# A graph layer with a mixture of experts on one core: a chunk of four windows moved from the end of the chunk list to its front, a short chain for every chunk of four, weights loaded in order of use, slot work per edge tile capped

## Chip, cores and metric

One NeuronCore of a Trainium2 chip runs the whole program in one launch. The metric is the device time of one execution in microseconds (us), median of the timed runs. Beside the timed runs one further execution was recorded by the hardware profiler; all durations of single instructions come from it.

## What is computed

6250 nodes with 256 features each, 100,000 edges sorted by destination, 8 experts of which each node uses 2. Cut to what matters:

```python
h = layernorm(x)
agg = segment_sum(h[src], dst) / max(deg, 1)            # mean over incoming edges
x = x + concat([h, agg], axis=1) @ gnn_W.T + gnn_b
xn = layernorm(layernorm(x)) * gamma + beta
logits = xn @ Wr + br
w = softmax(top_k(logits, 2))                           # two experts for each node
for e in range(8):
    y += (gelu(xn @ W1[e] + b1[e]) @ W2[e] + b2[e]) * w_full[..., e]
x = x + y
```

All data and all matmuls are fp32. The expert matrices are 256 x 512 and 512 x 256.

## The kernel before, in words

**Early stage.** The kernel first computes, for all nodes, a matrix `z_d` (normalised features times the neighbour half of the graph weights, with 8 router columns) and then, in steps spread over the first edge tiles (`u_stages`), `u_d` (the own half, with the residual). Both are kept in DRAM.

**Edge phase.** The sorted edges are cut into W = 56 windows of C = 14 edge tiles of P = 128 edges, 784 tiles in all. For an edge tile, POOL gathers the 128 source rows of `z_d` into one of XG = 16 `xg` tiles (`gather`, L594); DVE makes a one-hot matrix of the destinations for seven tiles at a time (`hot_tiles`, L605); PE adds the tile into the window's sums with one fp32 matmul, which the records show as two (`add_edges`, L611). Gathers are written 16 tiles ahead, so a gather waits only until the matmul 16 tiles before it has released its `xg` tile. A window's first row may be shared with the window before it: the sums go to DRAM and one row comes back (`put_sums`, `share_row`), and DVE adds it (`shared_row`, L617).

**From sums to expert slots.** Four windows make a group. When a group's sums are there, a fixed chain of steps runs on DVE, ACT and PE: normalisation, router logits, rank of the experts, one-hot slots (`one_hot_slots`, L686/L687), a matmul that sorts the tokens (`sort_tokens`, L694), and for the chunk the positions of each window's run of tokens of each expert (`share_runs`, `place_runs`, `tile_experts`). ACT then copies the runs into a slot buffer `xe` (`copy_runs`, L809); there are two of them, taken in turn, and each is cleared once by DVE when it is first used (L797). At which edge tile after the group's end each step is written is set by the class `Steps`: there is a long form and a short form. In the long form the copies begin 37 tiles after the last window and the experts (`placed`) 50 tiles after it for a chunk of four windows, 62 for a chunk of eight; in the short form they begin 23 and 32 tiles after it for a chunk of four. Only the last two chunks use the short form.

**Chunks and experts.** The windows are grouped into chunks of TG = 4 or CW = 8 windows. A chunk is what the experts work on at a time. With eight windows each expert has 256 slots, with four 128, and one slot task then takes two experts; three extra tiles of 128 slots (XT) take what doesn't fit. `expert_stages` returns a chunk's slot tasks as a list of (planned us, function): `hidden` (L825, 1.8 or 2.0 us), `result` (L840, 1.75 us), and `one`, `two`, `three` (L857, L866, L875; 1.7, 0.5 and 1.75 us) for the extra tiles. Results go to `y_d` in DRAM.

**The order of the work** on all engines is that of the program, written by hand[...]. `after(t)` is called behind each edge tile t. It writes the steps that fall due at t, then takes slot tasks from the list `tasks` until the budget `rate` (planned us per edge tile) is used up, then lets `sum_rows` write row sums. `start_experts` sets `rate` when a chunk's experts become ready: the planned us in the list divided by the tiles left until the chunk's `deadline`. When the last chunk becomes ready, the rate is 2.0. After the last edge tile the same function is called with t = 784, 785 and so on until nothing is left.

**Row sums.** `sum_rows` gathers, for one window, each token's two expert results from `y_d` with two POOL gathers (`gather_rows`, L923), and later (6 planned us later, or when more than four wait) adds them on DVE (`add_rows`, L930) and stores the rows. It begins in the last 100 edge tiles, one window for every 12 planned us, faster in the last 16 tiles; after the last edge tile it is one window for every 2.4 planned us, but a window only once its chunk's slot tasks have all been written. From the last 16 tiles on, the row sums use the `xg` tiles as buffers.

**Weights.** When the last step of `u_stages` has been written (edge tile 38), its memory is given to the pool `slots`, and the 16 weight loads of 512 KB (eight of `w1`, then eight of `w2`) are issued on ACT's queue, one for every two tiles from tile 40.

The chunk list is one line (L77), the planner's parameters one line each:

```python
sizes = [TG] + [CW] * ((W - 4 * TG) // CW) + [TG] * 3
...
nw, short = chunks[index][1], index >= len(chunks) - 2
...
rate = max(rate, 1.01 * total / (deadline(L.index) - now))
...
spent = min(spent + rate, rate) if tasks else 0.0
```

Of the kernel before, what the change touches and what calls it, by code (L numbers as in the profile page):

```python
# [8 lines left out]
F32 = mybir.dt.float32  # L9
# [8 lines left out]
P = 128  # L18
EPS = 1e-5
C = 14  # L20
TB = 4
UB = 2
TG = 4
CW = 8
# [7 lines left out]
def gnn_ffn_kernel(ctx: ExitStack, tc: tile.TileContext, x, x_cols, src, dst, gw, gw_t, gb, gb_cols, gamma, beta,  # L32
# [30 lines left out]
    nc = tc.nc  # L63
    N, D = x.shape
    E = src.shape[0]
    NX, H = w1.shape[0], w1.shape[2]
    KD, KH = D // P, H // P
# [3 lines left out]
    W = -(-E // EW)  # L71
# [2 lines left out]
    DZ = D + NX  # L74
    DA = DZ + 1
    HR = NT * P
    sizes = [TG] + [CW] * ((W - 4 * TG) // CW) + [TG] * 3  # L77
    assert sum(sizes) == W
    chunks = [(sum(sizes[:i]), n) for i, n in enumerate(sizes)]

# [8 lines left out]
    def slot_number(nw):  # L89
        return more_at(nw) + XT * P  # L90

    SC = slot_number(CW) + CAP
# [410 lines left out]
    def weights(pool):  # L503
        w1_sb = pool.tile([P, NX, KD, H], F32, name="w1_sb", bufs=1)
        w2_sb = pool.tile([P, NX, KH, D], F32, name="w2_sb", bufs=1)
        parts = [(w1_sb[:, e], w1[e].rearrange("(k p) h -> p k h", p=P)) for e in range(NX)]
        parts += [(w2_sb[:, e], w2[e].rearrange("(k p) d -> p k d", p=P)) for e in range(NX)]
        return w1_sb, w2_sb, parts

    xg = [edges.tile([P, DA], F32, name=f"xg{i}") for i in range(XG)]  # L510
# [97 lines left out]
    def add_edges(V, c):  # L608
        if c == 0:
            V.pS = ps.tile([P, DA], F32, name="pS")  # L610
        nc.tensor.matmul(V.pS, V.hot[c // HC][:, c % HC, :], xg[(V.g * C + c) % XG],  # L611
                         start=(c == 0), stop=(c == C - 1))
# [179 lines left out]
    def copy_runs(K, e, j0, nw):  # L792
        if e == 0 and j0 == 0:
            assert K.index < 2 or Ks[K.index - 2].left == 0
            if K.index < 2:
                xe.append(slots.tile([P, KD, SC], F32, name=f"xe{K.index}", bufs=1))
                nc.vector.memset(xe[-1], 0.0)  # L797
            K.xe = xe[K.index % 2]
        _, v = nc.values_load_multi_w_load_instructions(
            K.runs[0:1, e, j0:j0 + nw, :].rearrange("o j t -> o (j t)"), engines=(ET.Activation,),  # L800
            min_val=0, max_val=slot_number(K.nw), skip_runtime_bounds_check_because="clamped to it")
        for i in range(nw):
            j = j0 + i
            src_at = nc.s_assert_within(v[2 * i + 1], 0, 2 * P,
                                        skip_runtime_bounds_check_because="a window has so many at most")
            whole = xs[:, j * KD * 2 * P:(j + 1) * KD * 2 * P + CAP]
            src = bass.AP(tensor=whole.tensor, offset=whole.offset,
                          ap=[whole.ap[0], [2 * P, KD], [1, 2 * P + CAP]])
            nc.scalar.activation(K.xe[:, :, bass.ds(v[2 * i], CAP)], src[:, :, bass.ds(src_at, CAP)], AF.Copy)  # L809

    def expert_stages(K):

# [126 lines left out]
    tasks, later, xe, Ks, sums, adds = [], {}, [], [], [], []  # L939
    slots, w1_sb, w2_sb = None, None, None  # L940
    now, spent, rate, clock, due, spares = None, 0.0, 0.0, 0.0, 0.0, 0
    ends = [(first + n) * C - 1 for first, n in chunks]

    class Steps:
# [1 line left out]


        def __init__(self, index):
            nw, short = chunks[index][1], index >= len(chunks) - 2
            if short:  # L950
                self.x1, self.var, self.roots, self.norms = 2, 4, 5, 7
                self.route, self.exps, self.weigh, self.choices, self.count = 8, 10, 11, 12, 14
                self.hot, self.sort, self.each, self.tiles, self.copied, self.pace = 17, 20, 1, 17, 23, 1
            else:
                self.x1, self.var, self.roots, self.norms = 3, 6, 8, 11
                self.route, self.exps, self.weigh, self.choices, self.count = 12, 15, 17, 18, 22
                self.hot, self.sort, self.each, self.tiles, self.copied, self.pace = 25, 29, 2, 27, 37, 1.5
            self.placed = self.copied + int(NX * nw // TG * self.pace) + 1
# [3 lines left out]
    def deadline(index):  # L962

        if index + 1 == len(chunks):
            return None
        t = ends[index + 1] + steps_of[index + 1].placed
        if chunks[index][1] > chunks[index + 1][1] or index == len(chunks) - 3:
            t = ends[index + 2] + steps_of[index + 2].copied - 4
        return t

    def at(t, f, *args):
        later.setdefault(max(t, now), []).append(lambda: f(*args))
# [36 lines left out]
    def start_experts(K):  # L1009
        nonlocal rate  # L1010
        tasks.extend(expert_stages(K))
        Ks.append(K)
        rate, total = 0.0, 0.0
        for L in Ks:
            total += sum(us for us, _, of in tasks if of is L)
            if L.left and deadline(L.index):
                rate = max(rate, 1.01 * total / (deadline(L.index) - now))
        if K.index == len(chunks) - 1:
            rate = 2.0
        sums.extend((K, j) for j in range(K.nw))  # L1020

    def sum_rows():

        nonlocal due
        while adds and (adds[0][0] <= clock or not (sums or tasks)):
            adds.pop(0)[1]()
        left = W * C - 1 - now
        while sums and not sums[0][0].left and clock >= due and left < 100:
            if 0 < left < XG and spares + 3 > XG - left:
                return  # L1030
            K, j = sums.pop(0)
            V = Group()
            gather_rows(K, j, V)
            adds.append((clock + 6.0, lambda K=K, j=j, V=V: add_rows(K, j, V)))
            while len(adds) > 4:
                adds.pop(0)[1]()
            due = clock + 12.0 if left >= XG else max(due, clock - 6.0) + (4.0 if left > 0 else 2.4)

    def after(t):
        nonlocal now, spent, clock  # L1040
        now = t
        while later.get(t):
            later[t].pop(0)()
        later.pop(t, None)
        clock += 0.6 if t < W * C else 0.3
        spent = min(spent + rate, rate) if tasks else 0.0
        while tasks and spent > 0:
            us, f, _ = tasks.pop(0)
            spent -= us
            clock += us  # L1050
            f()
        sum_rows()

    def new_window(g, V_before):
        V = Group()
        V.g, V.before, V.hot = g, V_before, []
        hot_tiles(V, 0)
        return V
# [7 lines left out]
    for index, (first, nw) in enumerate(chunks):  # L1066
        K = Group()
        K.index, K.first, K.nw, K.groups = index, first, nw, []
        K.count = work.tile([1, 2, CW, NX], F32, name="count")
        for g in range(first, first + nw):  # L1070
            if g % TG == 0:
                G = Group()
                G.n, G.first, G.x1 = TG, g, []
                G.mv = small.tile([P, TG, 2], F32, name="mv4", bufs=2)
                K.groups.append(G)
            if g > 0:
                V = V_next
            for c in range(C):
                t = g * C + c
                add_edges(V, c)  # L1080
                if c == 0:
                    hot_tiles(V, HC)
                if c == HC and g + 1 < W:
                    V_next = new_window(g + 1, V)
                if t + XG < len(edge_tiles):
                    gather(*edge_tiles[t + XG])
                for to, what in loads[:1]:
                    loads.pop(0)
                    nc.sync.dma_start(to, what)
                if u_tasks and t % 2 == 0:  # L1090
                    u_tasks.pop(0)()
                    if not u_tasks:
                        u_pools.close()
                        slots = fast_pools.enter_context(tc.tile_pool(name="slots", bufs=2))
                        w1_sb, w2_sb, parts = weights(slots)
                        for n, (to, what) in enumerate(parts):
                            at(t + 2 + 2 * n, nc.scalar.dma_start, to, what)
                if c == HC + 5:
                    load_u(V)
                if c == C - 1:  # L1100
                    window_done(V, G, K, t)
                after(t)
    t = W * C
    while later or tasks or sums or adds:
        after(t)
        t += 1
# [8 lines left out]
    with tc.If(wrong_r > 0), tc.tile_pool(name="gp", bufs=1) as gp:  # L1115
        w1_sb, w2_sb, parts = weights(gp)
# [130 lines left out]
```

## Time and profile before

| What | us |
|---|---|
| timed runs, median of 3 (lowest, highest) | 1456.79 (1456.22, 1457.76) |
| the profiled execution's own time | 1251.55 |
| its span, first to last instruction | 1249.6 |
| PE busy with matmuls | 1081.8 (87%) |
| POOL busy | 866.3 (69%) |
| first and last edge gather (L594) | 72.4 and 1087.5 |
| first and last edge matmul (L611) | 83.6 and 1112.5 |
| last slot matmul begins (L875) | 1222.9 |

The profiled execution is 205 us shorter than the median of the timed runs. A time inside the program can only be read from the profiled one. A line of a group of instructions gives the source line, engine, operation, output and input by their names, the count, the busy time and the mean duration of one in ns, then the idle time of the engine just before these instructions and what ended most of it. "issue" means that the profile shows nothing that was waited for. A line of a timeline gives start, duration and instruction, and in brackets the idle time before it and what ended it. The granted clock is that of PE, 1.00 being full speed; its mean in this execution was 0.95.

### The profile page before, as it was taken

What the parts mean: (1) busy time and instruction counts of PE and PEld (TensorE: products, weight loads), DVE (VectorE), ACT (ScalarE), POOL (GpSimd) and SP (SyncE); (2) the same over time, 40 slices, a digit from 0 to 9 for tenths busy, and PEclk for the clock granted to TensorE, in tenths of its full rate; (3) what the DMA queues carried; (4) which work ended last, traced back from release to release, by engine and by line L of the source; (5) the groups of instructions that cost most, each with busy time, mean ns of one, the idle gap of its engine ahead of it and who ended that gap; (6) DMA issues with size and microseconds to landing.
All of it is one profiled execution on the core that took longest, in us unless ns stands there. A gap on an engine that the chain in (4) does not pass through costs nothing. (4 is left out here: it accounts for less than half of the span.)

```text
span 1249.6 us, 17771 instructions
## 1 busy us (share of the span) xinstructions
PE 1081.8 (87%) x4806; PEld 869.3 (70%) x4806; DVE 684.6 (55%) x2137; ACT 446.0 (36%) x1155; POOL 866.3 (69%) x915
## 2 busy tenths in 40 slices
PE   6998746787869999999999999899999898997881
PEld 5877535665648887677768777787768776885670
DVE  6766647543746276634746275534734647348452
ACT  2510003521273236433373236433363424433520
POOL 3057777777777777777777777777777776656672
PEclk9999978898999999999999999999999998998896
DMA  9989895455554555555555555555555665656673
GB/s 287 350 293 310 268 363 135 129 155 137 142 144 135 155 157 156 150 148 144 151 152 150 151 145 156 146 152 143 150 152 151 165 179 138 159 174 198 199 222 108
DMA packets 140272, 221.74 MB, mean 177 GB/s; under 512 B 23316, under 2 KB 107615, under 8 KB 140038
## 3 DMA queue, kind: packets, MB, share of 16 engines
q0 software_dynamic: 43104, 120.94, 37.3%
q1 hardware_dynamic: 88726, 90.15, 22.2%
q10 hardware_dynamic: 8336, 9.45, 2.2%
q8 instruction: 41, 0.67, 0.2%
q14 instruction: 65, 0.53, 0.1%
HBM read 166.29 MB, written 54.20 MB: 176 GB/s over the span
## 5 line engine op out<-in xcount | busy, mean ns | idle before, releaser
L594 POOL DMA_INDIRECT xg<-z_d,src_i x784 | 745.0, 950 | 287.5 <-issue 115.7
L611 PE MATMUL pS<-xg,hot 128*128 128x265 f32 x1568 | 441.9, 404 | 63.1 <-DMA xg<-z_d,src_i 35.7
L611 PEld LDWEIGHTS pS<-xg,hot 128*128 128x128 f32 x1568 | 294.3, 196 | 156.7 <-DMA xg<-z_d,src_i 69.7
L825 PE MATMUL ph<-xe,w_sb 128*128 128x256 f32 (+1 forms) x1152 | 226.9, 349 | 23.9 <-ACT xe L809 23.9
L825 PEld LDWEIGHTS ph<-xe,w_sb 128*128 128x128 f32 x1152 | 193.3, 203 | 47.7 <-ACT xe L809 26.8
L840 PE MATMUL py<-w_sb,hid 128*128 128x256 f32 x896 | 213.0, 382 | 4.4 <-DVE rows L844 4.3
L840 PEld LDWEIGHTS py<-w_sb,hid 128*128 128x128 f32 x896 | 170.2, 191 | 30.7 <-DVE rows L844 6.4
L832 ACT ACTIVATE hid<-ph,b_sb 128x256 f32<-128x256 f32 (+1 forms) x288 | 103.4, 426 | 234.3 <-PE ph L825 234.1
L605 DVE TENSOR_TENSOR hot<-cols,rel 128x896 f32<-128x896 f32 x112 | 121.0, 1081 | 86.8 <-PE pS L611 84.1
L809 ACT ACTIVATE xe<-xs x448 | 139.4, 311 | 62.8 <-ACT xe L809 31.0
L923 POOL DMA_INDIRECT xg<-y_d,rows_i x92 | 89.1, 969 | 60.2 <-issue 20.9
L697 ACT ACTIVATE xs<-pm,beta_sb,gamma_sb 128x256 f32<-128x256 f32 x112 | 57.1, 561 | 112.0 <-PE pm L694 112.0
L844 DVE TENSOR_TENSOR rows<-py,b_sb 128x512 f32<-128x512 f32 x56 | 38.5, 688 | 97.6 <-PE py L840 97.6
L621 ACT ACTIVATE sums<-pS 128x265 f32<-128x265 f32 x56 | 21.7, 388 | 167.8 <-issue 56.4
L617 DVE TENSOR_TENSOR pS<-pS,row 1x265 f32<-1x265 f32 x55 | 23.4, 426 | 92.4 <-PE pS L611 76.7
L694 PE MATMUL pm<-to,xn 128*128 128x256 f32 x224 | 59.0, 387 | 10.5 <-DVE end L757 4.9
L256 PE MATMUL ph<-gc,x_t 128*128 128x264 f32 (+1 forms) x200 | 57.5, 413 | 10.5 <-DVE u_t L415 6.3
L930 DVE SCALAR_TENSOR_TENSOR xg<-xg,w,xg 128x256 f32<-128x256 f32 x92 | 44.0, 483 | 38.6 <-DMA xg<-y_d,rows_i 22.2
L857 PE MATMUL ph<-w_sb,xe 128*128 x108 | 56.5, 649 | 7.2 <-DVE rows L861 6.7
L832 ACT ACT_TABLE_LOAD x23 | 29.5, 1283 | 79.8 <-PE ph L825 79.5
L875 PE MATMUL py<-w_sb,hid 128*128 x216 | 52.2, 385 | 6.1 <-ACT hid L869 3.3
L694 PEld LDWEIGHTS pm<-to,xn 128*128 128x128 f32 x224 | 42.1, 192 | 20.6 <-issue 12.8
(190 smaller groups left out, 919.5 us busy)
## 6 DMA issues: line engine op xcount, KB each, us to landing
y_d<-rows SPq DMA_DIRECT2D x56, 256.0 KB
xg<-z_d,src_i POOLq DMA_INDIRECT x784, 2.9
w_sb<-w_dram ACTq DMA_DIRECT2D x16, 512.0 KB
sums_d<-sums SPq DMA_DIRECT2D x55, 132.5 KB
x<-u_d SPq DMA_DIRECT2D x55, 132.0 KB
x_d<-x SPq DMA_DIRECT2D x56, 128.0 KB
u_d<-u_t SPq DMA_DIRECT2D x24, 264.0 KB
x_t<-x_cols_dram SPq DMA_DIRECT2D x12, 512.0 KB
```

What stands on the lines that cost most here:

```text
L256: nc.tensor.matmul(pz, x_t[:, t, k, :], gc[:, h * KD + k, :n], start=(k == 0), stop=(k == KD - 1))
L594: nc.gpsimd.indirect_dma_start(out=xg[(g * C + c) % XG][:, :DZ], out_offset=None, in_=z_d[:, :], in_offset=bass.IndirectOffsetOnAxis(ap=sr ...
L605: nc.vector.tensor_tensor(hot, col[:, None, :].to_broadcast([P, HC, P]), V.rel[:, c:c + HC, None].to_broadcast([P, HC, P]), op=ALU.is_equal)
L611: nc.tensor.matmul(V.pS, V.hot[c // HC][:, c % HC, :], xg[(V.g * C + c) % XG], start=(c == 0), stop=(c == C - 1))
L694: nc.tensor.matmul(px[:, k, :], G.xn[i][:, k * P:(k + 1) * P], G.one_hot[i], start=True, stop=True)
L697: nc.scalar.activation(xs[:, at:at + 2 * P], px[:, k, :], AF.Identity, bias=beta_sb[:, k:k + 1], scale=gamma_sb[:, k:k + 1])
L809: nc.scalar.activation(K.xe[:, :, bass.ds(v[2 * i], CAP)], src[:, :, bass.ds(src_at, CAP)], AF.Copy)
L825: nc.tensor.matmul(ph[:, i, a * S:(a + 1) * S], w1_sb[:, U.e + a, k, c * P:(c + 1) * P], K.xe[:, k, (U.e + a) * S:(U.e + a + 1) * S], star ...
L832: nc.scalar.activation(U.hid[:, c, a * S:(a + 1) * S], ph[:, i, a * S:(a + 1) * S], AF.Gelu, bias=b1_sb[:, U.e + a, c:c + 1])
L840: nc.tensor.matmul(U.py[:, h, :], U.hid[:, c, h * P:(h + 1) * P], w2_sb[:, U.e + h * UE // 2, c, :], start=(c == 0), stop=(c == KH - 1))
L857: nc.tensor.matmul(ph, K.xe[:, k, at:at + P], w1_sb[:, bass.ds(T.e, 1), k, :].rearrange("p a h -> p (a h)"), start=(k == 0), stop=(k == KD ...
L923: nc.gpsimd.indirect_dma_start(out=V.y2[r], out_offset=None, in_=y_d[K.index][:, :], in_offset=bass.IndirectOffsetOnAxis(ap=G.rows[:, r, i ...
```

## The change

The chunk list becomes two chunks of four, five of eight, two of four; before it was one of four, five of eight, three of four. Every chunk of four uses the short form of `Steps`. The weight loads are issued in the order w1[0], w1[1], w2[0], w1[2], w2[1] and so on, on the same queue behind the same tiles. The two clears of the slot buffers leave `copy_runs` and are written 4 and 12 tiles behind the end of `u_stages`. The rate is limited to 0.72 planned us per edge tile, and behind the last edge tile the budget is 2.0 per step from the start.

```diff
-    sizes = [TG] + [CW] * ((W - 4 * TG) // CW) + [TG] * 3
+    sizes = [TG] * 2 + [CW] * ((W - 4 * TG) // CW) + [TG] * 2
...
-        parts = [(w1_sb[:, e], w1[e].rearrange("(k p) h -> p k h", p=P)) for e in range(NX)]
-        parts += [(w2_sb[:, e], w2[e].rearrange("(k p) d -> p k d", p=P)) for e in range(NX)]
+        first = [(w1_sb[:, e], w1[e].rearrange("(k p) h -> p k h", p=P)) for e in range(NX)]
+        second = [(w2_sb[:, e], w2[e].rearrange("(k p) d -> p k d", p=P)) for e in range(NX)]
+        parts = first[:1]
+        for e in range(NX):
+            parts += first[e + 1:e + 2] + second[e:e + 1]
...
     def copy_runs(K, e, j0, nw):
         if e == 0 and j0 == 0:
             assert K.index < 2 or Ks[K.index - 2].left == 0
-            if K.index < 2:
-                xe.append(slots.tile([P, KD, SC], F32, name=f"xe{K.index}", bufs=1))
-                nc.vector.memset(xe[-1], 0.0)
             K.xe = xe[K.index % 2]
...
+    def clear_slots():
+        xe.append(slots.tile([P, KD, SC], F32, name=f"xe{len(xe)}", bufs=1))
+        nc.vector.memset(xe[-1], 0.0)
...
-            nw, short = chunks[index][1], index >= len(chunks) - 2
+            nw, short = chunks[index][1], chunks[index][1] < CW
...
-                rate = max(rate, 1.01 * total / (deadline(L.index) - now))
-        if K.index == len(chunks) - 1:
-            rate = 2.0
+                rate = max(rate, 1.01 * total / max(1, deadline(L.index) - now))
+        rate = min(rate, 0.72)
...
-        spent = min(spent + rate, rate) if tasks else 0.0
+        pace = rate if t < W * C else 2.0
+        spent = min(spent + pace, pace) if tasks else 0.0
...
                         for n, (to, what) in enumerate(parts):
                             at(t + 2 + 2 * n, nc.scalar.dma_start, to, what)
+                        for n in range(2):
+                            at(t + 4 + 8 * n, clear_slots)
```

## The prediction

> **Words used.** An edge tile is one of the 784 groups of 128 edges; the kernel is written tile by tile, and behind each tile go some "slot tasks" (the expert matmuls of an earlier chunk). Windows are the 56 groups of 14 tiles. "Units" are the planner's own microseconds for slot tasks (`expert_stages`), 510.7 in all: 41.85 for a chunk of 4 windows, 68.65 for one of 8. The tail is what is written behind the last edge tile, in steps numbered on from 784.
>
> **What bounds the kernel now.** I read the page's engine line and groups first, then the busy time by stretches, then POOL's timeline near the end, then the waits after the last edge tile.
>
> ```profile
> PE 1081.8 (87%) x4806; PEld 869.3 (70%) x4806; DVE 684.6 (55%) x2137; ACT 446.0 (36%) x1155; POOL 866.3 (69%) x915
> ...
> L594 POOL DMA_INDIRECT xg<-z_d,src_i x784 | 745.0, 950 | 287.5 <-issue 115.7
> L611 PE MATMUL pS<-xg,hot 128*128 128x265 f32 x1568 | 441.9, 404 | 63.1 <-DMA xg<-z_d,src_i 35.7
> ...
> L923 POOL DMA_INDIRECT xg<-y_d,rows_i x92 | 89.1, 969 | 60.2 <-issue 20.9
> ```
>
> PE looks like the bound, but POOL's 69% leaves out the 0.30 us ahead of each gather. The stretches show it (columns: us, then busy time and instructions of PE, PEld, DVE, ACT, POOL, then clock, DMA share, GB/s).
>
> ```profile
> 150.00:200.00 50.00, 28.49 (x96) 21.34 (x95) 27.15 (x94) 6.24 (x13) 37.85 (x40) 0.76 0.91 303
> ...
> 800.00:850.00 50.00, 48.71 (x224) 41.70 (x223) 22.02 (x58) 13.71 (x28) 37.81 (x40) 1.00 0.55 150
> ...
> 1050.00:1100.00 50.00, 48.74 (x268) 41.15 (x267) 24.85 (x77) 23.57 (x76) 30.71 (x33) 1.00 0.56 150
> ...
> 1200.00:1250.00 50.00, 19.22 (x72) 13.12 (x70) 16.94 (x35) 3.43 (x12) 21.29 (x23) 0.76 0.51 151
> ```
>
> POOL makes 40 gathers per 50 us, one per 1.25 us, from 100 us to 1000 us without a break, whether PE is busy (800) or not (150). So POOL paces the edge phase, and PE work can be moved about in it for nothing. At 1050 POOL is down to 33: there PE holds it. POOL's timeline says where:
>
> ```profile
> 1087.52 0.95 POOL L594 DMA_INDIRECT xg<-z_d,src_i  x1 [0.30 <-PE pS L611]
> 1089.65 0.95 POOL L923 DMA_INDIRECT xg<-y_d,rows_i  x1 [1.19 <-PE pS L611]
> ...
> 1104.88 0.96 POOL L923 DMA_INDIRECT xg<-y_d,rows_i  x1 [2.11 <-PE pS L611]
> ...
> 1110.52 0.94 POOL L923 DMA_INDIRECT xg<-y_d,rows_i  x1 [2.17 <-PE pS L611]
> ...
> 1229.23 0.94 POOL L923 DMA_INDIRECT xg<-y_d,rows_i  x1 [11.55 <-DMA y_d<-rows]
> ```
>
> The last edge gather is at 1087.5, the last edge matmul at 1112.5 (its line's last start): PE is 25 us behind, and the row-sum gathers into the same `xg` tiles wait for it. Then the tail, POOL at one gather per 1.25 us again up to 1217, and the last chunk: its experts start at 1174.7, PE ends at 1224.9, the last four windows' gathers go at 1229 to 1239.
>
> [...] the next gather follows by 0.30 us, while the y gathers land 3.6 us (median) after issue. So 1.25 us is POOL's own time. [...] the tail shows "DVE xg <- DMA xg<-y_d" for 22.2 us. [...]
>
> **The change part by part.** The total is unchanged: four chunks of 4 and five of 8 either way, so no matmul, gather or copy is added. Units are honest: a `result` of 1.75 units shows 8 matmul records in 1.73 us, a two-expert `hidden` of 2.0 shows 1.78; a chunk of 4 is about 39.7 us of PE, one of 8 about 67.4, so 0.95 to 0.98 of the units.
>
> *Where slot work goes.* I worked the rates through by the code's own formulas. Before: experts start at tile 105 at 0.34 units a tile; from 229 0.62; from 677 1.0; from 759 1.27. By the last edge tile 431.0 units are done, 37.9 are queued and 41.9 come with the last chunk. After: start at 87 with the cap 0.72, from 143 0.30, from 285 0.62, from 733 0.72. Done by tile 676: 325.3 against 316.5; by the last edge tile 395.7, so 73.2 queued plus 41.9. The head start is 8.8 units; beyond that, 35.3 units move from the last 100 edge tiles into the tail.
>
> *Start.* An earlier start at 87 to 143 costs PE 0.445 (edge tile) + 0.70 + 0.085 (sort) = 1.23 us a tile, under POOL's 1.25: nothing, hidden by POOL. The 16 weight loads keep ACT's queue and tiles 40 to 70, only their order changes; the first need (about 195 us) comes after their issue (149 to 179 us): nothing. The two clears (L797, 4.3 us each) move from tiles 92 and 204 to 42 and 50 on DVE, ahead of the one-hot tiles, where DVE already waits 11.1 us for a row. Behind them queue L617 and L605, and PE behind these. Cover is the 16 gathered tiles, 20 us: I take 0, the other end +9. The short chain puts chunk 0's and 1's DVE and ACT steps into 32 steps in place of 50; PE and DVE have room (28 and 27 of 50 us), 0.
>
> *Edge phase end.* POOL unhindered, with 20 row-sum gathers among the edges (10 windows): 72.4 + 783 x 1.25 + 20 x 1.25 = 1076; measured 1087.5, so 11 us were PE's doing. After: 9 windows by the same arithmetic, PE at 1.23 never behind: 1074 for the last gather, 1078 for the last edge matmul. That is 35 us early.
>
> *Tail.* PE has 35.3 units x 0.97 = 34 us more in it. Taken by PE alone: 1078 + 62.9 units until step 815 (61) + sort and counts (5) = 1144 for the last chunk's start, + 52 units (50) + some 5 idle = 1199. But POOL: 94 row-sum gathers are left, in place of 92, and 34 windows are written between tile 777 and step 815. The add follows about three windows later: 31 x 2.5 + 1.25, plus stalls like the 12 us of before (76 gathers from 1110.5 to 1217.7 took 107 in place of 95) in proportion, 9, plus landing 3.6: 1075 + 91 = 1166 before DVE is through to the copies. (The same sum for before: 1110.5 + 50 + 6 + 3.6 = 1170; measured 1174.7.) Windows go on to step 825: DVE there at about 1075 + 106 + 12 + 4 = 1197, PE one item (about 5 us) ahead, then 32 units (31 us) without row sums. PE ends between 1192 + 31 = 1223 and, if adds hold it less, 1213; I take 1219 for 1224.9. The drain after it (24.7 us: last writes, eight gathers, store) stays.
>
> **Sum.** -6 us: 1251.6 to about 1245.6 in the profiled execution. The median of the timed runs is 1456.8, 205 us above the profiled one, and no view shows why. I carry the difference over in us, since both explanations I can price keep it near: if the 205 us lie outside the loop, -6 stays. If PE ran at some 0.75 of its clock, PE would bound tiles 285 to 784: the edge phase saves 44.1 units (those done from 677 on) x 0.97 / 0.75 = 57, the early stretch costs 7 (56 tiles at 1.64 in place of 1.25, minus what 229 to 285 gets back), the tail grows by 45: -5. So **1451**.
>
> **Rivals.** (a) *PE free of POOL in the tail*: adds don't hold PE; end at 1199 in place of 1224.9, -26, **1431**. For it: py and rows buffers let PE lead a little; against: before's start at 1174.7 fits POOL's sum. (b) *Slower: POOL is the timed runs' bound.* If the 205 us lie in the 896 gathers (0.23 us each, 1.48 in all), POOL's pace with row sums is 1.8 us a tile, above even before's 1.5 to 1.76 of PE: there is no 25 us backlog to remove, the last edge comes 3 us earlier only, and 34 us of PE work plus three windows stand behind the row sums: after 31 units at the end in place of 12, and three windows x 3.0: +28, **1485**. It decides once the backlog that the cap removes is under about 28 us; the profile has 36 (25 + 11). (c) *Same*: DVE is at 1197 as worked out and PE finishes at 1223 to 1226: **1456**, within 0.2%. (d) *Early stall*: the clears delay the one-hot tiles until POOL's 16 tiles run out, +9 less the gain: **1460**.
>
> **Chances.** Forecast, 1440 to 1453.8: 0.47; (a) 0.12; (c) 0.17; (d) and like small losses 0.12; (b) 0.12. A difference of 0.2% (2.9 us) is about what this measurement can tell from none. Faster 0.59, same 0.17, slower 0.24. The forecast's own range is 1440 to 1453.8; the range that leaves out (b) and the far end of (a) is 1437 to 1470.
>
> **What would show it.** Right: last L594 near 1074 and last L611 within 5 us of it; POOL 40 per 50 us up to there; no "<-PE pS L611" ahead of the first L923; experts of the last chunk from about 1165; PE busy nearly without a gap after 1197; drain as before. Wrong: POOL under 40 per 50 us around 150 to 200 (clears); the last edge matmul well after 1080 (PE behind at 0.72); last chunk's start near 1175 or later.

## The result, and the profile after

| | before | after |
|---|---|---|
| timed runs, median of 4 each | 1456.51 us (1442.55 to 1457.76) | 1476.55 us (1465.74 to 1482.05) |

The ratio is 1.0144, with a 95% interval of 1.0095 to 1.0192: 20 us slower, where 6 us faster was forecast.

The 205 us between the profiled execution of before and its timed runs belong to the chip on which a kernel runs: the unchanged kernel takes 1457 us on one chip (A below; by their times, the timed runs above and the profile named "after" come from it) and 1251 us on another (B). On B the changed kernel takes 1279.72 us against 1251.80, ratio 1.0219 (1.0189 to 1.0248), which is +28 us. So profiles are compared here only between chips of the same pace. The profile shown of before stands for B; on which chip it was made isn't known, but the profile of `loads_clears` below, made on B and as fast as before, has the same four stages to about 1 us. The page of after on A:

```profile
PE 1156.3 (78%) x4806; PEld 916.2 (62%) x4806; DVE 683.7 (46%) x2137; ACT 444.4 (30%) x1155; POOL 865.8 (59%) x915
...
L597 POOL DMA_INDIRECT xg<-z_d,src_i x784 | 745.6, 951 | 472.5 <-issue 173.8
L614 PE MATMUL pS<-xg,hot 128*128 128x265 f32 x1568 | 447.9, 417 | 47.2 <-issue 39.0
```

and of the same kernel on B (line numbers are those of the changed kernel, 3 or 4 higher than before's):

```profile
PE 1088.4 (85%) x4806; PEld 866.8 (68%) x4806; DVE 684.2 (54%) x2137; ACT 446.0 (35%) x1155; POOL 867.3 (68%) x915
...
L597 POOL DMA_INDIRECT xg<-z_d,src_i x784 | 746.0, 952 | 303.2 <-issue 115.2
L614 PE MATMUL pS<-xg,hot 128*128 128x265 f32 x1568 | 446.9, 407 | 76.3 <-DMA xg<-z_d,src_i 53.5
...
L927 POOL DMA_INDIRECT xg<-y_d,rows_i x94 | 91.0, 969 | 72.9 <-DMA y_d<-rows 30.3
```

The counts are those of before but for two row-sum gathers (94 for 92, and two fewer into `y`), and the busy times too: no work was added. On B the idle time before the edge gathers grew from 287.5 to 303.2 us. The busy time by stretches says where (B, the windows shown of before and the one ahead of them):

```profile
100.00:150.00 50.00, 42.19 (x172) 33.54 (x171) 35.12 (x94) 0.79 (x2) 34.75 (x37) 0.95 0.85 264
150.00:200.00 50.00, 27.91 (x89) 20.77 (x87) 35.86 (x104) 5.96 (x12) 35.24 (x38) 0.78 0.91 301
...
1050.00:1100.00 50.00, 44.91 (x191) 37.96 (x192) 30.77 (x105) 22.29 (x60) 37.81 (x41) 0.90 0.58 158
...
1200.00:1250.00 50.00, 44.16 (x249) 36.86 (x249) 18.50 (x37) 13.12 (x47) 19.34 (x21) 0.97 0.50 156
```

POOL makes 37 and 38 gathers in the first two, where before it made 40; at 1050 it makes 41, where before it was held down to 33; at 1200 PE is still at work, where before it was nearly done. POOL's timeline at the two joints of the tail:

```profile
1098.37 0.95 POOL L597 DMA_INDIRECT xg<-z_d,src_i  x1 [0.31 <-issue]
1099.62 0.95 POOL L927 DMA_INDIRECT y<-y_d,rows_i  x1 [0.30 <-DMA xg<-z_d,src_i]
...
1257.30 0.94 POOL L927 DMA_INDIRECT xg<-y_d,rows_i  x1 [29.00 <-DMA y_d<-rows]
```

The wait for PE ahead of the first row-sum gather is gone, as forecast, but the last edge gather comes at 1098, not at 1074. Cut at edge gathers 285 and 677 (counted from 0), the last edge matmul and the last slot matmul, the time goes as follows (us in each stage, the first of them from the first edge gather on, read off POOL's and PE's timelines; the last two cuts are the starts of the last group of each):

| stage | before, B | after, B | difference | before (`b0`), A | after, A | difference |
|---|---|---|---|---|---|---|
| gathers 0 to 285 | 361.0 | 381.3 | +20.3 | 414.8 | 434.8 | +20.0 |
| gathers 285 to 677 | 491.0 | 491.5 | +0.5 | 577.4 | 576.5 | -0.9 |
| gather 677 to last edge matmul | 188.1 | 166.0 | -22.1 | 219.5 | 201.4 | -18.1 |
| to last slot matmul | 110.4 | 141.3 | +30.9 | 138.2 | 167.1 | +28.9 |

Both chips say the same: 20 us are lost at the start, and the end loses 9 to 11 where it should have won 6. (On A a single execution scatters: the profiled one of `b0`, the kernel before run once more, took 1451.7 us, its median is 1459.5.)

### The profile page after: what moved, and what is told of

Read it like the earlier page. It is cut to its first block, busy times and chain, and to the rows that moved or that the text cites. A ratio compares the mean times of both kernels' runs of the same rounds, so it can differ in the third digit from the quotient of the medians.

```text
span 1479.5 us, 17770 instructions
## 1 busy us (share of the span) xinstructions
PE 1156.3 (78%) x4806; PEld 916.2 (62%) x4806; DVE 683.7 (46%) x2137; ACT 444.4 (30%) x1155; POOL 865.8 (59%) x915
## 5 line engine op out<-in xcount | busy, mean ns | idle before, releaser
L597 POOL DMA_INDIRECT xg<-z_d,src_i x784 | 745.6, 951 | 472.5 <-issue 173.8
L614 PE MATMUL pS<-xg,hot 128*128 128x265 f32 x1568 | 447.9, 417 | 47.2 <-issue 39.0
L614 PEld LDWEIGHTS pS<-xg,hot 128*128 128x128 f32 x1568 | 317.2, 206 | 131.2 <-issue 69.2
L829 PE MATMUL ph<-xe,w_sb 128*128 128x256 f32 (+1 forms) x1152 | 232.8, 351 | 48.5 <-ACT xe L809 19.6
L844 PE MATMUL py<-w_sb,hid 128*128 128x256 f32 x896 | 237.2, 407 | 34.3 <-issue 30.7
L844 PEld LDWEIGHTS py<-w_sb,hid 128*128 128x128 f32 x896 | 182.8, 206 | 69.3 <-issue 34.5
L809 ACT ACTIVATE xe<-xs x448 | 139.3, 311 | 60.2 <-issue 29.5
L697 PE MATMUL pm<-to,xn 128*128 128x256 f32 x224 | 66.4, 420 | 49.9 <-DVE to L690 16.4
L879 PE MATMUL py<-w_sb,hid 128*128 x216 | 60.5, 430 | 30.8 <-DVE rows L883 20.6
L861 PE MATMUL ph<-w_sb,xe 128*128 x108 | 61.7, 701 | 28.5 <-DVE rows L865 19.5
L879 PEld LDWEIGHTS py<-w_sb,hid 128*128 128x128 f32 x216 | 44.8, 215 | 43.5 <-ACT xe L809 17.8
```

The lines of the kernel that those rows point to most:

```text
L597: nc.gpsimd.indirect_dma_start(out=xg[(g * C + c) % XG][:, :DZ], out_offset=None, in_=z_d[:, :], in_offset=bass.IndirectOffsetOnAxis(ap=sr ...
L697: nc.tensor.matmul(px[:, k, :], G.xn[i][:, k * P:(k + 1) * P], G.one_hot[i], start=True, stop=True)
L829: nc.tensor.matmul(ph[:, i, a * S:(a + 1) * S], w1_sb[:, U.e + a, k, c * P:(c + 1) * P], K.xe[:, k, (U.e + a) * S:(U.e + a + 1) * S], star ...
L844: nc.tensor.matmul(U.py[:, h, :], U.hid[:, c, h * P:(h + 1) * P], w2_sb[:, U.e + h * UE // 2, c, :], start=(c == 0), stop=(c == KH - 1))
L861: nc.tensor.matmul(ph, K.xe[:, k, at:at + P], w1_sb[:, bass.ds(T.e, 1), k, :].rearrange("p a h -> p (a h)"), start=(k == 0), stop=(k == KD ...
L879: nc.tensor.matmul(py[:, 0, :], T.hid[:, c, :P], w2_sb[:, bass.ds(T.e, 1), c, :].rearrange("p a d -> p (a d)"), start=(c == 0), stop=(c == ...
```

## The experiments

Two theories of the loss stood at first. *Start*: the early slot work of the first chunk makes PE wait in front of the edge matmuls, POOL's 16 tiles run out, and every later gather shifts. *Tail*: what the cap pushes behind the last edge tile costs more than it saves. A third, that the loss belongs to the chip, had to go first. `rate`, `placed`, `short` and `sizes` are those of the diff. Each run is compared with the kernel before on its own chip.

### On chip A: is it the chip, and is it the cap?

`b0` is the kernel before, unchanged.

> The kernel before, unchanged, to have its profile in the condition of its timed runs (about 1456 us) and not only the 1251 us one. Ratio to itself 1.00. If PE's waits of the kind 'issue' come with that condition and not with the change, they are some 300 to 400 us here too (74 us in the 1251 us profile, 360 us in the changed kernel's). If the change brings them, they stay under 100 us and the time under 1300.

Measured: 1459.51 us, ratio 1.0008 (0.9982 to 1.0034). `chunks_only` is before with the new list and the short chain:

```diff
-    sizes = [TG] + [CW] * ((W - 4 * TG) // CW) + [TG] * 3
+    sizes = [TG] * 2 + [CW] * ((W - 4 * TG) // CW) + [TG] * 2
...
-            nw, short = chunks[index][1], index >= len(chunks) - 2
+            nw, short = chunks[index][1], chunks[index][1] < CW
```

> Only the chunk list and the short chain of the kernel after; weights, clears and budget as before. Theory START (the early, short chain of the first chunk stalls the edge tiles): slower than before by 10 to 25 us. Theory TAIL (the cap moves 34 us of PE work behind the last edge tile, where it isn't hidden): within 0.4% of before.

Measured: 1480.55 us, 1.0156 (1.0108 to 1.0203). `after_nocap` is after with before's budget:

```diff
-        rate = min(rate, 0.72)
+        if K.index == len(chunks) - 1:
+            rate = 2.0
...
-        pace = rate if t < W * C else 2.0
-        spent = min(spent + pace, pace) if tasks else 0.0
+        spent = min(spent + rate, rate) if tasks else 0.0
```

> The kernel after with the budget rule of before (no cap at 0.72, 2.0 only once the last chunk is ready). START: as slow as the kernel after, +15 to +25 us on before, the clears adding up to 9 of them. TAIL: within 0.4% of before, since the last edge tiles again take the slot work.

Measured: 1472.51 us, 1.0105 (1.0066 to 1.0144). `after_again` is the changed kernel.

> The kernel after, on the same chip as the three others: +1.0% to +1.9% on before, as in the first measurement.

Measured: 1478.80 us, 1.0154 (1.0103 to 1.0204). So the loss is there without cap, clears and weight order (`chunks_only`), and stays without the cap (`after_nocap`). What the cap is worth on A can't be told: the intervals of 1.0105 and 1.0154 overlap.

What chip A's profiles have more of is waits. PE's waits of before on B, then of after on A (us in all, times, longest):

```profile
PE pS L611 <- issue: 7.2, 3, 3.9
```

```profile
PE pS L614 <- issue: 39.0, 38, 5.8
PE py L844 <- issue: 30.7, 33, 1.8
...
PE ph L829 <- issue: 17.1, 23, 4.2
```

All such waits of PE and its weight loads are 360 us in after on A against 74 in the profile of before. `b0` shows the same on A: 286 us of them, and 1.47 us per edge gather against 1.25 (gathers 285 to 677). "issue" names nothing that was waited for. Both kernels have it on A, and on B, where the changed kernel has 82 us of it and before 74, the loss is no smaller, so it is no cause of the difference between them.

### On chip B: one part at a time

`short_first` is before with the short chain for the first chunk, which puts its experts at tile 87 in place of 105:

```diff
-            nw, short = chunks[index][1], index >= len(chunks) - 2
+            nw, short = chunks[index][1], index == 0 or index >= len(chunks) - 2
```

> The kernel before with one change: the first chunk takes the short chain too (experts from tile 87 at 0.30 units a tile; chunk list, weights, clears and budget as before). Theory CHAIN (PE stands behind steps of the chain whose DVE and ACT work isn't done when PE reaches them, while the weights load): 10 to 25 us slower, edge gather 171 some 15 to 25 us later after the first gather than in the kernel before (248 us). Theory RATE (the 0.72 to 0.755 units a tile of the first chunk put PE behind the gathers): within 0.4% of before.

Measured: 1267.26 us, 1.0129 (1.0102 to 1.0156), +16 us; gathers 0 to 285 take 376.8 us, the other three stages are before's within 1 us. `list_only` is before with the new list alone (the `sizes` line above; the first two chunks in the long chain, 0.755 planned us a tile).

> Only the chunk list of the kernel after; the first two chunks keep the long chain (experts from tile 105, 0.755 units a tile until 158, then 0.34). CHAIN: within 0.4% of before. RATE: 10 to 25 us slower, lost between edge gathers 121 and 190.

Measured: 1264.91 us, 1.0117 (1.0096 to 1.0137), +14; in its profile 8 in the first stage and 8 in the last. Neither theory had the second half of that. `slow_start` is `chunks_only` with 0.45 planned us a tile for the first two chunks:

```diff
+        if K.index < 2:
+            rate = 0.45
```

> Chunk list and short chains as in chunks_only, but 0.45 units a tile for the first two chunks. CHAIN: as slow as chunks_only, +1.0% to +2.0%. RATE: at most +0.5% on before, since 0.45 is under the 0.62 that the middle runs at.

Measured: 1275.85 us, 1.0188 (1.0168 to 1.0209). A slower rate doesn't cure the short chain's start: gather 120 comes 171.1 us after the first, as in `short_first` (170.1), against 152.6 in before. Its 24 us are the 16 of `short_first` and the 8 that `list_only` loses in the last stage. `loads_clears` is before with the new order of the weights and the moved clears alone.

> The kernel before with only the weights in order of use and the two clears moved to tiles 42 and 50. If the clears stall the one-hot tiles: +0.3% to +0.6%. Otherwise within 0.3% of before, with the first hidden matmul at the same time.

Measured: 1250.93 us, 1.0001 (0.9988 to 1.0015): nothing, either way, in before's long chain. `after_third` is the changed kernel on B.

> The kernel after once more, for a chip on which the kernel before takes 1251 us, if it is one; on any chip by its difference to before on the same chip. By the runs so far: the early short chain 16 us, the chunk list 13 us without a cap; if the cap neither helps nor harms, +24 to +30 us in all. On a 1251 us chip the forecast's edge phase should show: last edge gather 1002 us after the first (before: 1015) plus the 16 us lost at the start.

Measured: 1279.72 us, 1.0219 (1.0189 to 1.0248); its profile is the one read above.

The start of `short_first`, PE first, then ACT's first copy, then POOL:

```profile
198.81 3.84 PE L611 MATMUL pS<-xg,hot 128*128 128x265 f32 x16
216.77 3.78 PE L825 MATMUL ph<-xe,w_sb 128*128 128x128 f32 x16 [14.12 <-ACT xe L809]
220.34 3.33 PE L611 MATMUL pS<-xg,hot 128*128 128x265 f32 x12
```

```profile
202.89 1.34 ACT L809 ACTIVATE xe<-xs  x4 [3.73 <-DVE q L780]
```

```profile
197.21 0.94 POOL L594 DMA_INDIRECT xg<-z_d,src_i  x1 [3.29 <-PE pS L611]
...
208.82 0.95 POOL L594 DMA_INDIRECT xg<-z_d,src_i  x1 [0.30 <-issue]
221.71 0.94 POOL L594 DMA_INDIRECT xg<-z_d,src_i  x1 [11.94 <-PE pS L611]
```

And the same place in before:

```profile
224.58 3.78 PE L825 MATMUL ph<-xe,w_sb 128*128 128x128 f32 x16 [10.28 <-ACT xe L809]
```

```profile
226.28 0.95 POOL L594 DMA_INDIRECT xg<-z_d,src_i  x1 [0.30 <-issue]
229.52 0.94 POOL L594 DMA_INDIRECT xg<-z_d,src_i  x1 [2.29 <-PE pS L611]
```

In both, PE reaches the first `hidden` matmul before ACT has copied the slots (`xe`, L809: eight groups of four copies, one group per 1.76 us) and stands in front of edge matmuls whose tiles are there (14.12 us in `short_first`, 10.28 in before). Two things differ. PE stands 3.8 us longer in `short_first`, where it arrives before the first copy has begun, and POOL has less room. In before PE stands from 214.3, POOL goes on for ten more gathers, up to 226.28, and loses 2 us. In `short_first` PE stands from 202.65, and until then it had itself been late: POOL had waited 3.29 us for it at 197.21, with all 16 tiles in use. So POOL has room for five more gathers, stops after that of 208.82 and loses 11.6 us. Nothing gives that back: POOL paces the next 500 tiles, and gathers 285 to 677 take before's 491 us to within 1.

The first copy itself waits for DVE, which has the 4.33 us clear of the slot buffer (L797) in front of that step. In the changed kernel the clear has been moved away from there, and the wait is shorter (`after_third`):

```profile
216.29 3.78 PE L829 MATMUL ph<-xe,w_sb 128*128 128x128 f32 x16 [10.69 <-ACT xe L809]
```

POOL loses 7.8 us at this place, where `slow_start`, with the same list and chain but the clear in its old place, loses 11.6. So the moved clear, worth nothing in before's chain (there PE's wait falls from 10.28 to 6.94 us in `loads_clears`, and POOL had lost only 2 us to it), seems to take part of the harm out of the short one; no run changes it alone there.

### Is it the wait, and is the ring too small?

`short_late` is `short_first` with the first chunk's experts at tile 105 again:

```diff
+            if index == 0:
+                self.placed = 50
```

> short_first with the experts of the first chunk written from tile 105, as in the kernel before, instead of tile 87; the short chain itself stays. If PE standing at the first hidden matmul until ACT's eight copies are through is the cause: the 16 us are gone, within 0.3% of before. If the count and sort steps of the short chain cost it: still 10 to 16 us slower.

Measured: 1255.55 us, 1.0026 (1.0016 to 1.0036): 13 of the 16 us are gone with that one number; the short chain's steps on DVE and ACT cost the other 3 (1.39, 1.59 and 1.31 us of idle on POOL at 193 to 198 us). The first `hidden` doesn't wait there. PE still stands once for 7.16 us, at 211.4, in front of an edge matmul: its one-hot matrix is late, since DVE waits 9.31 us for a step of ACT that is queued behind the copies. POOL has eight free tiles then and loses nothing. With 20 `xg` tiles in place of 16 (XG), for before and for `short_first`:

> The kernel before with 20 gathered tiles in place of 16. The start has stalls of 2 us only, so little to win there; at the end PE may fall 25 us behind before POOL stalls, and row sums find four tiles more: between 0 and -0.7%.

> short_first with 20 gathered tiles. If the loss is cover used up: against b0_xg20 on the same chip 10 to 12 us slower (short_first: 16 against before), the loss at edge gathers 86 to 120 down by 5. If the short chain costs time that no cover hides: 16 again.

These and two runs below were made on a third chip, where before takes 1251.77 us. Measured: `b0_xg20` 1254.61 us, 1.0024 (1.0014 to 1.0034), `short_xg20` 1267.66 us, 1.0127 (1.0104 to 1.0150). The longer ring alone makes before 3 us slower, where a gain or nothing was expected. Between the two runs lie 13 us, with an interval of about 3 us either way, so the time alone doesn't decide between the 10 to 12 of the one theory and the 16 of the other. The lines of `short_xg20`, PE and then POOL:

```profile
217.98 3.78 PE L825 MATMUL ph<-xe,w_sb 128*128 128x128 f32 x16 [14.88 <-ACT xe L809]
```

```profile
222.65 0.94 POOL L594 DMA_INDIRECT xg<-z_d,src_i  x1 [11.94 <-PE pS L611]
```

The same 11.94 us. POOL had filled the longer ring as well shortly before, at 199: when PE stands still, from 203.10, six of the 20 tiles are free, where five of the 16 were, and PE stands 0.8 us longer. The four tiles more saved only the small waits ahead of it (3 us). So the depth of the ring is the wrong measure of cover; what counts is how many tiles are free at that moment.

### The rate at the start, and the chunk list

`list_slow` is `list_only` with 0.5 planned us a tile for the first two chunks (the lines of `slow_start` with another number).

> list_only with 0.5 units a tile for the first two chunks (0.755 and 0.34 before). If the rate costs the 5 to 6 us at edge gathers 143 to 171, they are gone: +0.5 to +0.7% on before, all of it behind gather 677. If not: as list_only, +1.0 to +1.4%.

Measured: 1257.67 us, 1.0052 (1.0033 to 1.0071). Gathers 0 to 285 take 359.3 us, before's pace; so some 7 of `list_only`'s 14 us were the rate (each run against before on its own chip). Where it costs, in `list_only`, PE and then POOL:

```profile
289.90 1.12 PE L866 MATMUL ph<-ident,rows 128*128 128x128 f32 x4 [4.72 <-DVE rows L861]
291.01 3.78 PE L875 MATMUL py<-w_sb,hid 128*128 x8
294.58 2.09 PE L611 MATMUL pS<-xg,hot 128*128 128x265 f32 x6
```

```profile
288.52 0.95 POOL L594 DMA_INDIRECT xg<-z_d,src_i  x1 [0.30 <-issue]
295.94 0.95 POOL L594 DMA_INDIRECT xg<-z_d,src_i  x1 [6.48 <-PE pS L611]
```

At that rate the chunk's last tasks stand close together; one waits 4.72 us for DVE (`rows`, L861), and the edge matmuls stand behind it. PE does no edge matmul from 285.2 to 294.6; 13 of the 16 tiles are in use when that begins, and POOL's third gather after it, at 288.52, is the last that has room. It loses 6.2 us. `list_slow` has no wait of over 0.4 us on POOL there. The other 7 us stay at the end (last edge matmul to last slot matmul 118.2 us in `list_slow`, 118.0 in `list_only`, 110.4 in before). `list_end` tests what the list does there, with all four small chunks last and no early start at all:

```diff
-    sizes = [TG] + [CW] * ((W - 4 * TG) // CW) + [TG] * 3
+    sizes = [CW] * ((W - 4 * TG) // CW) + [TG] * 4
...
-    for n in {CW, sizes[0]}:
+    for n in {CW, TG}:
```

(The second pair of lines keeps a clear of the buffer `xs` as it is in before.)

> The kernel before with the chunk of four moved the other way: five chunks of eight, then four of four (experts from tile 173). Theory AVAILABLE (after tile 677, where row sums slow POOL to 1.5 us a tile, PE needs slot work at hand; the new list has only 33 units there, before 69 and more): this list has 57 units at tile 677 and the last chunks early, so from edge gather 677 on it needs no longer than before (325 us), within 3 us, and the late start of the experts costs nothing, since PE work is hidden by POOL until then: within 0.4% of before, maybe 0.3% faster. Theory HEAD START (what counts is how much is done at tile 677): 327.9 units against 316.5, so 8 to 11 us faster.

Measured: 1253.29 us, 1.0007 (0.9993 to 1.0022): the first experts start at tile 173, 68 tiles after before's, and it costs nothing. A head start is worth nothing here: 11 planned us more are done at tile 677 than in before, and no time is won. What fits the runs is how much slot work is ready when the row sums slow POOL to some 1.4 us a tile (80 us for 56 tiles in before, 78 in `list_only`; 57 planned us are ready in `list_end`, none of it lost). Between gathers 677 and 733, first before and then `list_only`:

```profile
924.00:1004.00 80.00, 74.13 (x320) 61.74 (x319) 39.66 (x135) 35.88 (x90) 60.50 (x65) 0.96 0.58 158
```

```profile
932.00:1010.00 78.00, 63.66 (x244) 47.34 (x245) 43.49 (x144) 27.30 (x68) 59.12 (x62) 0.91 0.56 153
```

POOL is about equally busy in both (60.50 and 59.12 us), PE does 10 us less in `list_only`: in the planner's arithmetic only 33 planned us are ready there, since the next chunk of eight becomes ready at tile 733, where before the fifth one was ready at 677. That work comes back behind the last edge tile. No run varied the ready work alone, so this reading is argued from the three lists and not shown by itself.

### The cap on the new list

`list_cap` is `list_only` with the cap and the tail budget of the change; `list_cap90` has 0.9 for 0.72.

> The chunk list and the budget rule of the kernel after (cap 0.72, then 2.0), but the first two chunks with the long chain; weights and clears as before. The forecast's tail sum (35 us won at the last edge tile, 29 lost behind it) would give -6 us on before; list_only's loss of 6 us at edge gathers 143 to 171 stays, so about 0. If the cap only moves work to where it isn't hidden: +15 to +25 us.

> list_cap with 0.9 for 0.72: 64.3 units queued behind the last edge tile in place of 73.2 (list_only 45.9, before 37.9). If the loss in the tail goes with these units it lies between list_only and list_cap; if PE is held by POOL's row sums there, all three are equal within 3 us.

Measured: 1263.86 us, 1.0088 (1.0065 to 1.0111), and 1269.27 us, 1.0118 (1.0088 to 1.0149), beside 1.0117 of `list_only`. In `list_cap` the stage from gather 677 to the last edge matmul is 22 us shorter than in `list_only` and the stage after it 21 longer: the cap moves work and time by the same amount. The +11 to +12 us of `list_cap` lie between its two expectations, and 0.9 is not better than 0.72; within their intervals the three are equal. The cap alone on before's list was not run: by the planner's arithmetic a slot buffer would then be filled again before its earlier chunk is done.

### Do the parts add up?

`after_late` is after with `placed = 50` for the first chunk (the edit of `short_late`). `after_mend` is after with both losses of the start taken out:

```diff
-            nw, short = chunks[index][1], chunks[index][1] < CW
+            nw, short = chunks[index][1], index >= len(chunks) - 2
...
-        rate = min(rate, 0.72)
+        rate = 0.5 if K.index < 2 else min(rate, 0.72)
```

> The changed kernel with one number changed: the experts of the first chunk start 50 tiles behind its last window, as in the long chain, not 32; its DVE and ACT steps keep the short chain. Theory: of the 28 us that the change costs, 12 to 16 come from PE reaching the first hidden matmul before ACT's copies are done while POOL's 16 tiles are already used up. Then the first chunk's wait goes, gathers 86 to 120 take about 46 us in place of 55, and the time is 12 us below the changed kernel's 1279.7: 1268, or +16 us over before. Rival, the 0.72 planned us a tile: the same work now stands closer together, the loss only moves to tiles 105 to 171, and the time stays within 4 us of 1279.7.

> The changed kernel with the long chain for the first two chunks and 0.5 planned us a tile while they are worked on; list, weight order, clears and the 0.72 later as in the change. Theory: the costs add up; with both losses of the start gone, gather 677 comes within 3 us of where it comes before (852 us behind the first), and what is left is the chunk list's 7 us in the tail: 1258.5, ratio 1.0055. Rival, the cap: with its work pushed behind the last edge tile it costs more once the start is mended, up to the forecast's 31 us in the tail against 22 won in the edge phase: 1262 to 1266. Rival, the forecast: with the start mended the change is worth its 6 us: 1246.

Both ran on A, where before took 1461.13 us. Measured: `after_late` 1476.75 us, 1.0113 (1.0066 to 1.0159); `after_mend` 1465.83 us, 1.0049 (1.0028 to 1.0071). The second is what the sum of the parts said (1.0055), above the forecast's gain and below the rival's 1.008: with the start mended what is left of the change is a loss of 5 us by the medians, 7 by the ratio, about that of the list. The profile doesn't confirm it by place: `after_mend`'s gather 677 comes 12 us later than `b0`'s, where 3 were expected; with executions that scatter by 10 us on this chip that says little either way. `after_late` settles less: +16 us over before, as expected, but after itself is only +20 to +22 on A, and its 86th to 120th gathers take 49.2 us for 59.5 (the first `hidden` no longer waits 11.11 us for the copies), of which over a third is lost again by tile 285. Whether 6 or 12 us were saved lies within its interval.

No version made here beats the kernel before.

## Why the prediction was wrong, step by step

**POOL paces the edge phase: right** on B and the third chip (491 us for 392 gathers in every kernel). On A (577 to 582) it is right between spells in which POOL stands as well as PE, mostly with free tiles at hand (ahead of 59 of the 62 late gathers of after). **"PE work can be moved about in it for nothing": wrong.** It holds for PE's busy time, not for PE's order. In `short_first` PE stood 14.12 us before the slot matmul at 216.77, and the edge matmuls written behind it, with their tiles there, began only at 220.34.

**Start, the step that failed.** "1.23 us a tile, under POOL's 1.25: nothing, hidden by POOL" was put at 0 and measured +20 us. The sum added durations and left out the wait for ACT's copies, which the trace of before had (10.28 us at 224.58), and took a slack of 0.02 us a tile for enough to catch up. One at a time on before, the parts are 16 us for the short chain's start at tile 87 (13 of them PE's wait, `short_late`) and 7 for the rate of 0.755 (`list_only` less `list_slow`). They don't simply add up. In after's own trace on B, what POOL idles beyond the usual 0.30 us ahead of gathers 86 to 285 is 4.5 us before the first `hidden`, 7.8 at it and 6.1 behind it, 18 in all, where before has 2 (the rest of the +20 lies ahead of gather 86, where `list_only`, up to there the same program as before, shows +4 as well). Of the 6.1, 5.1 are two waits at 282 and 296 us that `slow_start`, at 0.45, doesn't have. "PE and DVE have room" for the short chain, put at 0, was wrong by 3 in `short_late`. The weights at nothing were right, and so was the 0 taken for the clears on before's chain (`loads_clears`); with the short chain they seem to help. "Cover is the 16 gathered tiles, 20 us", said of the clears, has the wrong quantity: at the first `hidden` five were free.

**Edge phase end, mis-sized.** "35 us early" measured 22, counted from gather 677. From gather 677 to 783 153.5 us for 163.1, 10 of the 11 us that were PE's doing; and PE ends 12.5 us behind the last gather, where 4 were taken and before has 25. Why PE is still ten tiles behind at 0.72 no run isolates.

**Tail: the number was right, the reason less so.** 29 us more than before were forecast, 30.9 measured. But PE itself fills most of it: 73.2 + 41.9 queued units are 112 us at 0.97, PE is busy for 124 of the 141 us (on B, from 1111 on), and its waits for DVE's rows there are few (us in all, times, longest):

```profile
PE py L844 <- DVE rows L848: 12.2, 4, 4.6
PE py L879 <- DVE rows L883: 3.8, 6, 1.2
```

POOL and DVE, which the forecast let set the end, don't: POOL waits 29.00 us for the last `y_d` at 1257.30. How far an add that waits for its gather holds the work written behind it on DVE, on which the forecast's sum for the tail rests, no run shows by itself. Rival (a)'s picture of the tail, PE free of POOL, was nearer, without its gain.

**The sum**: forecast 0 - 35 + 29 = -6; measured on B +20.3 + 0.5 - 22.1 + 30.9 = +29.6 to the last slot matmul. Even without the start it would have been +9, as `after_mend` says for A with +5 to +7: the head start of 8.8 planned us, counted as a gain, is worth nothing (`list_end`), and the list leaves less work ready when POOL slows.

**Rivals.** (b) had the right side and near the right size for a wrong reason: on A, where a gather comes every 1.47 us in the mean, before's PE is still 24 us behind the last gather (1261.67 and 1286.06 in `b0`), since PE stands in spells there too; so the backlog it called missing is there. (d) put the loss in the right place, at the start, but on the clears. Of the two readings of the 205 us neither holds: they are not outside the loop (199 of `b0`'s 200 us lie in the four stages of the table), and PE's mean granted clock in `b0` is 0.90, not 0.75.

## What to carry to other kernels

When work is moved earlier in the order of a program, ask first when its inputs are ready and what is written behind it: in `short_first` PE stood 14.12 us for ACT's copies, and POOL lost 11.6. A busy time per tile below the pace of the bound (1.23 us under 1.25) was not enough. In these runs the ring of gathered tiles covered a wait only by the tiles that were free at that moment: with five free of 16 and six free of 20 the next gather came after the same 11.94 us, since PE had been late before and the longer ring was nearly full as well. Work that was hidden anyway gained nothing here by an earlier start (`list_end`, whose experts start 68 tiles later: 1.0007); what fits the runs is that enough of it must be ready where the bound slows down (33 planned us in `list_only`, 57 in `list_end`). And a part that is worth nothing alone, as the moved clear (1.0001 in `loads_clears`), can, it seems, be worth something beside another: POOL's loss at the first `hidden` was 7.8 us with it (`after_third`) and 11.6 without (`slow_start`).

## What the runs showed of the hardware

The same kernel, before, took 1457 us on one chip (A) and 1251 and 1252 on two others. On the first, PE's instructions come one at a time in some spells, here 0.74 and 1.40 us apart, with nothing that the profile shows as waited for (after on A):

```profile
612.44 0.46 PE L829 MATMUL ph<-xe,w_sb 128*128 128x256 f32 x1 [1.04 <-issue]
613.18 0.46 PE L829 MATMUL ph<-xe,w_sb 128*128 128x256 f32 x1 [0.28 <-issue]
614.58 1.11 PE L829 MATMUL ph<-xe,w_sb 128*128 128x256 f32 x4 [0.94 <-issue]
```

POOL stands in such spells too. Between gathers 285 and 677 most gathers come 1.25 us after the one before on both chips; in `b0` 58 of the 392 come 1.4 to 3.7 us after it, and these hold the whole difference of 86 us. In after on A it is 62 of them, and ahead of 59 the tile that the gather needs had been free for 2 us or more. Idle time ahead of the edge gathers is 472.5 us in after on A against 303.2 on B (with "issue" 173.8 and 115.2). The mean of a single instruction hardly moves (417 and 407 ns for the edge matmul, 951 and 952 ns for the gather): the time is between instructions. Its cause stays open. The loss of the change was 20 to 22 us in two comparisons on that chip and 28 on B, with intervals that overlap.
